# Paged attention behind per-sequence adapters: the order of the work ahead of the first step, and the adapter gathers of the first group, rearranged

## The chip, the cores and the metric

One core of a Trainium2 chip runs the whole kernel. The metric is the device time of one execution in microseconds (us). The kernel before takes 1193.76 us, the median of 3 runs (1192.11 to 1201.34).

## The reference, cut to what matters

There are 8 sequences of 128 tokens with 512 values each, all in float32. First a full 512x512 adapter matrix is picked for each sequence and its product is added; then comes one attention layer with 32 query heads on 8 key heads of 128 values, over 512 cached keys and the 128 new ones.

```python
x = x + einsum('bsi,boi->bso', x, weight[adapter_ids])         # 16 adapters of 512 x 512
q, k, v = x @ Wq.T, x @ Wk.T, x @ Wv.T                         # 32, 8 and 8 heads of 128
q, k = rope(rmsnorm(q, q_norm_w), pos), rope(rmsnorm(k, k_norm_w), pos)   # pos = seqlen + token
kc, vc = k_cache[block_table], v_cache[block_table]            # 16 pages of 32 rows per sequence
scores = q . [kc, k] / sqrt(128), cached keys at or past seqlen masked
x = x + softmax(scores) @ [vc, v] @ Wo.T
```

## The kernel before, in words

**Steps.** The heads are split into G = 4 groups of 2 key heads and 8 query heads. A step is one group of one sequence; 32 steps run in the order group by group, sequence by sequence (`steps`, L248). A step has 8 slots, one for each query head: its score product `sc` (L1040, two matmuls into one of two PSUM buffers), mask and row minimum on DVE (L1050), exponential on ACT (L1066), reciprocal on DVE (L1106), scaling on POOL (L1113), and a 32x32-block transpose on DVE (L886) whose result goes through an exchange of four DMAs on SP's queue (`exchange`, L803) to become `pT`. Between the score products, PE does the pieces of the list `main`: the value product `o` and output product `out` of the step before, and the projections `pj_kv`, `pj_q` of the step after. A planner gives each piece a cost and hands each slot an equal share of what is left (L1093 to L1100).

**Operands.** Every product needs both sides turned. In the first step that is done by PE: four 128x128 transposes into a PSUM buffer (`ps_mm`, four buffers; with `spare` the two score buffers), then a copy out by ACT or DVE (`turn_x` L550, `turn_weights` L492, `turn_lora` L529, `turn_lora_row` L542, `turn_x1` L553, `turn_kc` L756, `turn_k` L768, `turn_q` L787). Later q, k and weights go through DVE transposes and exchanges. `copy_k` (L775) copies the new keys on ACT out of the exchanged `qT` of the step to come; it stands ahead of that slot's exponential in ACT's order.

**Group 0 in particular.** The first eight steps also do the adapters. For step i, sequence i + 2 is turned in slot 0, its adapter in slots 0 to 3 (2 to 5 in step 0), its product `y` comes with `main` (`lora_y`, L587), the addition to the residual follows on DVE (L591), and the sum is turned again by `turn_x1`, registered with `at` for slot 8 of the step, which is slot 0 of the next (slot 9 in step 0). The adapter of sequence b + 3 is gathered by an indirect DMA of 1024 KB that POOL issues (`gather_lora`, L237), in slot 6 (L1128 to L1130) together with the load of x (`load_x`, SP's queue). It lands in a single buffer, the one that `turn_lora` reads. POOL also issues the gathers of cached keys (slots 3 and 5) and values (slots 6 and 7).

**Ahead of step 0** (L932 to L983) the order is written out by hand; each engine takes its own instructions in this order. Two small rows hold sequence lengths and inverse frequencies (the first), and block table, adapter numbers and norm weights (the second). `spread` (L387) brings a row to all partitions by a matmul with ones. `rope_angles` (L394) works the first on DVE; `row_rest` (L423) the second: it casts it, spreads it and makes `bt_f` and `lora_ix` on DVE and `wn` on ACT. From them come the index tables (`row_numbers`, `row_values` on POOL, `row_tables` for groups 1 to 3 on DVE), the sine and cosine (`rope_sin`, `rope_cos` on ACT) and `rope_table` (four DVE operations for keys, five for queries). `pending` is a list of work that follows a product (`rotate`, L644: squares on ACT, then products with the tables on DVE; `norm_scales`, L687: power on POOL, then scaling on ACT); `run(pending)` issues it. A PSUM buffer is read by one engine after the other: in the trace DVE's L664 starts only when ACT's squares of the same product are done.

The order of the hand-written part before, PE's view: the first row, x of sequence 0, value weights (kv 2, 3), key weights (kv 0, 1), the second row, the four adapter blocks, `y`, first query weights (q0 0, 1), q0 2, 3, x1 of sequence 0, second query weights q1 0, 1, `pj_kv`, `pj_q` 0, the cached keys (`turn_kc`), q1 2, 3, `pj_q` 1, x of sequence 1, its adapter, q, k, and then step 0.

Of the kernel before, what the change touches and what calls it, by code (L numbers as in the profile page):

```python
# [19 lines left out]
B = 8  # L20
# [3 lines left out]
D = 128  # L24
# [28 lines left out]
def lora_then_paged_attention(  # L53
# [204 lines left out]
    for i, (g, b) in enumerate(steps):  # L258
        if i == 0:
            at(i, 2, False, lambda: turn_q(0, 1))  # L260
            at(i, 7, False, lambda: turn_q(1, 0))
            for n, h in enumerate((7, 8, 9, 10)):
                at(i, h, False, lambda n=n: turn_weights(("o1", 0, n)))
        if i == last:
            at(i - 1, 6, False, lambda: turn_q(last, 0))
            at(i, 2, True, lambda: turn_q(last, 1))


        for j, n, slot in ((0, i - 1, 6), (1, i, 2)):
            if (i, 0) in by_pe and i:  # L270
                at(n, slot, bool(j), lambda i=i, j=j: turn_k(i, j), 1)
            elif i:
                at(n, slot + 1 - j, True, lambda i=i, j=j: copy_k(i, j), 0)
            elif j:
                at(n, slot, True, lambda: turn_k(0, 1), 1)
        if g == 0 and b + 2 < B:
            at(i, 0, True, lambda b=b: turn_x(b + 2))
            for c in range(KC):
                at(i, c if i else c + 2, False, lambda b=b, c=c: turn_lora(b + 2, c))
            at(i, 8 if i else 9, True, lambda b=b: turn_x1(b + 2))  # L280
    for turns in turns_at.values():
        turns.sort(key=lambda t: not t[0])

# [110 lines left out]
    def rope_angles():  # L394
        nc.vector.tensor_copy(row_f[:, 0:B], row_i[:, 0:B])
        row = spread(0)
        nc.vector.tensor_copy(len_f, row[:, 0:B])
        par_f = rope["par"] = const.tile([P, 1], FP, name="par_f")
        nc.vector.tensor_copy(par_f, par)
        pos = const.tile([P, B], FP, name="pos")  # L400
        nc.vector.tensor_scalar(pos, len_f, par_f, None, ALU.add)
        def temp(tag):
            n = 4 + GK if tag in ("q0", "tq0") else 4
            t = work.tile([P, n, D], FP, tag=tag, name=f"rope_{tag}")
            return t[:, 0:4, :].rearrange("p h (u d) -> p (h u) d", u=2)

        ang, turns, sin, cos = temp("q0"), temp("q1"), temp("tq0"), temp("sw")
        nc.vector.tensor_tensor(
            ang,
            pos.unsqueeze(2).to_broadcast([P, B, H2]),  # L410
            row[:, at_ivf : at_ivf + H2].unsqueeze(1).to_broadcast([P, B, H2]),
            ALU.mult,
        )
        nc.vector.tensor_scalar(turns, ang, 1.0 / (2 * math.pi), ROUND, ALU.mult, ALU.add)
        nc.vector.tensor_scalar(turns, turns, ROUND, None, ALU.subtract)
        for part in (TWO_PI_1, TWO_PI_2, TWO_PI_3):
            nc.vector.scalar_tensor_tensor(
                out=ang, in0=turns, scalar=-part, in1=ang, op0=ALU.mult, op1=ALU.add
            )
        nc.vector.tensor_scalar(ang, ang, PI_BELOW, -PI_BELOW, ALU.min, ALU.max)  # L420
        rope.update(ang=ang, sin=sin, cos=cos)

    def row_rest():  # L423

        nc.vector.tensor_copy(row_f[:, at_bt:at_wn], row_i[:, at_bt:at_wn])
        row = spread(1)
        nc.vector.tensor_copy(rows_of["bt_f"].rearrange("p c q -> p (c q)"), row[:, 0:NB])
        nc.vector.scalar_tensor_tensor(
            out=lora_ix,
            in0=row[:, NB : NB + B],  # L430
            scalar=float(HID // 4),
            in1=rope["par"].to_broadcast([P, B]),
            op0=ALU.mult,
            op1=ALU.add,
        )
        for n in range(2):
            lo = at_wn - at_bt + (1 - n) * D
            nc.scalar.copy(wn[:, n, :], row[:, lo : lo + D])
# [10 lines left out]
        nc.scalar.activation(cos, cos, AF.Sin)  # L449
        table_set(AF.Exp)  # L450

    def rope_table(n):
        sin, cos = rope["sin"], rope["cos"]
        if n == 0:


            nc.vector.tensor_scalar(wn[:, 0, :], wn[:, 0, :], -SCALE, None, ALU.mult)
        w1 = wn[:, n, 0:H2].unsqueeze(1).to_broadcast([P, B, H2])
        w2 = wn[:, n, H2:D].unsqueeze(1).to_broadcast([P, B, H2])
        nc.vector.tensor_tensor(SW[:, n, :, H2:D], sin, w1, ALU.mult)  # L460
        nc.vector.scalar_tensor_tensor(
            out=SW[:, n, :, 0:H2], in0=sin, scalar=-1.0, in1=w2, op0=ALU.mult, op1=ALU.mult
        )
        nc.vector.tensor_tensor(CW[:, n, :, 0:H2], cos, w1, ALU.mult)
        nc.vector.tensor_tensor(CW[:, n, :, H2:D], cos, w2, ALU.mult)

# [462 lines left out]
    on_act, on_vec = nc.scalar.copy, nc.vector.tensor_copy  # L931
    row_parts()  # L932
    table_set(AF.Sin)
    rope_angles()
    turn_x(0, on_act)
    for n in (2, 3, 0, 1):
        turn_weights(("kv", 0, n), on_act)
    rope_sin()
    row_rest()
    for j in range(4):  # L940
        turn_lora_row(0, j, (on_act, on_vec)[j % 2])
    row_numbers()
    for c in range(LC):
        gather_k(0, c)
    row_values()
    rope_cos()
    for _, f in lora_y(0):
        f()
    rope_table(1)
    for n in range(2):  # L950
        turn_weights(("q0", 0, n), on_act)
    flush()
    for n in range(2, 4):
        turn_weights(("q0", 0, n), on_act)
    turn_x1(0, on_vec)
    for n in range(2):
        turn_weights(("q1", 0, n), on_act)
    make_mask(0)
    for _, f in project(0, "kv"):
        f()  # L960
    rope_table(0)
    run(pending)
    for _, f in project(0, "q0"):
        f()
    run(pending)
    for j in range(GK):
        turn_kc(0, j, on_vec)
    for n in range(2, 4):
        turn_weights(("q1", 0, n), on_act)
    run(pending)  # L970
    for c in range(LC):
        gather_k(1, c)
    row_tables(range(1, G))
    for _, f in project(0, "q1"):
        f()
    turn_x(1, on_vec)
    for c in range(KC):
        turn_lora(1, c, on_vec if c % 2 else on_act, True)
    gather_lora(2)
    turn_q(0, 0, on_act)  # L980
    turn_k(0, 0, on_act)
    for _ in range(3):
        load_next()  # L983

# [2 lines left out]
    for i, (g, b) in enumerate(steps):  # L987
        s = st[i]
        main = []
        if i == 0:  # L990
            main += lora_y(1)

            def second(n):
                run(pending)
                if n == 2:
                    turn_x1(1)
                turn_weights(("o0", 0, n))

            main += [(4 * TR * (1 + n // 2), lambda n=n: second(n)) for n in range(3)]
            main += [(4 * TR, lambda: turn_weights(("o0", 0, 3)))]  # L1000
        early = i >= B - 2
        if i and not early:
            main += values(i - 1, 0)
# [25 lines left out]
        for h in range(8):  # L1029
# [86 lines left out]
            if i < last:  # L1116
# [8 lines left out]
                    gather_v(i + 1, c)  # L1125
                if h == 6:
                    pending.append(lambda i=i: make_mask(i + 1))
            if g == 0 and h == 6 and b + 3 < B:  # L1128
                load_x(b + 3)
                gather_lora(b + 3)  # L1130
            if 8 * i + h - 1 in turn_when:
                load_next()

# [57 lines left out]
```

## Time and profile before

| | |
|---|---|
| median of 3 runs | 1193.76 us (1192.11 to 1201.34) |
| the profiled execution | 1193.18 us, of which the span from first to last instruction is 1191.3 us |
| granted TensorE clock over the span | 0.999 |
| busy: PE, DVE, POOL, ACT | 1172.7, 743.9, 674.1, 534.0 us |
| DMA moved | 217.59 MB, mean 183 GB/s |
| first score product of step 0 | at 40.75 us |
| first score products of steps 1 to 6 | at 74.14, 116.13, 160.87, 201.33, 241.80 and 282.26 us |

How to read it: times are us from the first instruction. A busy PE is one that has a matmul in flight, also where the matmul runs at half clock; "A <- B: 2.4, 1, 2.4" in the table of waits is the time that A's engine stood idle until B was done, in total, how often, and the longest. A timeline row is start, duration, engine, line, operation, written tile <- read tiles, and in brackets the idle time before it.

### The profile page before, as it was taken

Reading aid. Unit: us, or ns where it says so; the run is one execution under the profiler, and the core shown is the slowest. Engines: PE = TensorE matmul, PEld = TensorE weight load, DVE = VectorE, ACT = ScalarE, POOL = GpSimd, SP = SyncE. Lnnn points to the kernel's source line nnn. Section 1 sums busy time; section 2 is a strip of 40 time slices with the busy share of each in tenths; the row PEclk is TensorE's granted clock in tenths of the full one; section 3 lists DMA queues with packets and bytes.
Section 4 is the critical chain, followed back from the end, with each engine's and each line's share of the span. In section 5 each row is a group of like instructions: output and inputs, shape, how many; then the busy total and the mean of one; then the engine's idle time right before and its main releaser. Section 6 shows DMA issues by size and latency. Waiting matters only on the chain.

```text
span 1191.3 us, 13375 instructions
## 1 busy us (share of the span) xinstructions
PE 1172.7 (98%) x3354; PEld 572.0 (48%) x3354; DVE 743.9 (62%) x1675; ACT 534.0 (45%) x1648; POOL 674.1 (57%) x780
## 2 busy tenths in 40 slices
PE   7899999999999999999999999999999999999998
PEld 4555454454444444444444444444444444444454
DVE  5566566565667676666666676676666656665651
ACT  4564444444444444444444444444444444444432
POOL 5565346455666565656655556565555656655540
PEclk9999999999999999999999999999999999999999
DMA  8277577766867977786777978766777875665642
GB/s 291 100 180 197 135 220 206 172 180 168 226 173 189 253 192 191 191 215 169 199 187 180 258 198 216 196 175 171 190 203 178 219 180 148 148 153 135 152 111 59
DMA packets 173952, 217.59 MB, mean 183 GB/s; under 512 B 19508, under 2 KB 112436, under 8 KB 172980
## 3 DMA queue, kind: packets, MB, share of 16 engines
q1 hardware_dynamic: 111072, 128.76, 46.8%
q10 hardware_dynamic: 49524, 48.12, 12.7%
q0 software_dynamic: 13280, 39.86, 10.4%
q8 instruction: 28, 0.46, 0.2%
q14 instruction: 48, 0.39, 0.1%
HBM read 80.74 MB, written 17.83 MB: 83 GB/s over the span
## 4 chain that ended last, share of the span: by engine, by line
PE 96%; POOL 1%; DMA 1%; ACT 1%; DVE 1%; issue 1%; DVEq 0%; ACTq 0%; POOLq 0%
PE sc L1040 23%; PE o L566 23%; PE pj_q L566 18%; PE out L566 18%; PE pj_kv L566 9%; PE y L566 2%; PE lw L481 1%; DMA lraw<-in_L_cond_weight_dram,lora_ix 1%; PE x L481 1%; PE wt_q L499 0%; PE wt_kv L499 0%; PE qt L793 0%; PE wt_o L499 0%; POOL kc L617 0%; POOL vc L617 0%
## 5 line engine op out<-in xcount | busy, mean ns | idle before, releaser
L1050 DVE CUSTOM_DVE_ANT_0 p<-sc,mask 128x640 f32<-128x640 f32 x256 | 210.9, 824 | 381.2 <-PE sc L1040 380.9
L1066 ACT ACTIVATE p<-p,mn 128x640 f32<-128x640 f32 x256 | 212.0, 828 | 331.8 <-DVE mn L1050 328.0
L1113 POOL TENSOR_SCALAR p<-p,rc 128x640 f32<-128x640 f32 x252 | 201.5, 800 | 235.3 <-DVE rc L1106 230.9
L1040 PE MATMUL sc<-kT,qT 128*128 128x512 f32 (+1 forms) x1024 | 319.5, 434 | 1.1 <-ACT kT L773 0.8
L1040 PEld LDWEIGHTS sc<-kT,qT 128*128 128x128 f32 x1024 | 192.7, 191 | 232.5 <-issue 225.7
L566 PE MATMUL pj_q<-w_q,x1T 128*128 128x512 f32 x512 | 236.8, 593 | 0.7 <-ACT w_q L500 0.7
L566 PE MATMUL o<-pT,vc 128*128 128x512 f32 x512 | 237.1, 593 | 0.0
L566 PE MATMUL out<-w_o,oT 128*128 128x512 f32 (+1 forms) x528 | 234.9, 580 | 0.9 <-ACT oT L853 0.7
L886 DVE STREAM_TRANSPOSE tp<-p 128x640 f32<-128x640 f32 x252 | 210.8, 837 | 4.0 <-POOL p L1113 3.8
L685 POOL TENSOR_TENSOR q<-q,sw 128x512 f32<-128x512 f32 (+1 forms) x89 | 96.6, 1086 | 98.8 <-DVE sw L668 98.6
L617 POOL DMA_INDIRECT kc<-in_L_cond_k_cache_dram,key_ix x128 | 130.7, 1021 | 32.7 <-issue 32.5
L617 POOL DMA_INDIRECT vc<-in_L_cond_v_cache_dram,val_ix x128 | 127.3, 995 | 31.2 <-issue 29.8
L566 PEld LDWEIGHTS out<-w_o,oT 128*128 128x128 f32 x528 | 95.7, 190 | 93.5 <-issue 85.4
L566 PEld LDWEIGHTS pj_q<-w_q,x1T 128*128 128x128 f32 x512 | 92.4, 190 | 92.7 <-issue 90.6
L698 ACT ACTIVATE q<-q,rs 128x128 f32<-128x128 f32 x256 | 81.8, 390 | 118.1 <-POOL q L685 102.2
L566 PEld LDWEIGHTS o<-pT,vc 128*128 128x128 f32 x512 | 92.2, 191 | 88.5 <-issue 86.4
L566 PE MATMUL pj_kv<-w_kv,x1T 128*128 128x512 f32 x256 | 116.6, 593 | 0.7 <-ACT x1T L483 0.7
L651 ACT ACTIVATE sq<-pj_q 128x128 f32<-128x128 f32 x256 | 70.6, 276 | 57.5 <-PE pj_q L566 41.6
L693 POOL TENSOR_TENSOR rs<-ss,mhalf 128x6 f32<-128x6 f32 x64 | 77.3, 1207 | 5.3
L566 PEld LDWEIGHTS pj_kv<-w_kv,x1T 128*128 128x128 f32 x256 | 46.0, 190 | 45.6 <-issue 44.7
L566 PE MATMUL o<-pT,vn 128*128 128x512 f32 x128 | 65.4, 593 | 0.0
L651 ACT ACTIVATION_READ_ACCUMULATOR sq<-pj_q 128x1 f32 x256 | 49.7, 194 | 0.0
(123 smaller groups left out, 811.5 us busy)
## 6 DMA issues: line engine op xcount, KB each, us to landing
pT<-tp SPq DMA_DIRECT2D x252, 320.0 KB, 6.1
kT<-tk SPq DMA_DIRECT2D x248, 64.0 KB, 2.9
qT<-tq SPq DMA_DIRECT2D x116, 96.0 KB, 2.7
qT<-tq SPq DMA_DIRECT2D x120, 64.0 KB, 4.0
st_q<-in_L_cond_Wq_dram ACTq DMA_DIRECT2D x24, 256.0 KB, 5.5
xw_q<-tw_q ACTq DMA_DIRECT2D x24, 256.0 KB, 5.5
st_o<-in_L_cond_Wo_dram ACTq DMA_DIRECT2D x24, 256.0 KB, 5.7
xw_o<-tw_o ACTq DMA_DIRECT2D x24, 256.0 KB, 6.5
```

Source lines behind the costliest of these rows:

```text
L481: nc.tensor.transpose(t[:, j, :], blk, ident)
L566: nc.tensor.matmul(y[0], lhsT=lhsT, rhs=rhs, start=(k == 0), stop=(k == len(pieces) - 1))
L617: nc.gpsimd.indirect_dma_start(out=dst[:, c, :], out_offset=None, in_=src, in_offset=bass.IndirectOffsetOnAxis(ap=rows[:, g, at : at + 1], ...
L651: nc.scalar.activation(sq, t[:, h, :], AF.Square, scale=float(D) ** -0.5, accum_out=ss[:, h : h + 1])
L685: add.tensor_tensor(dst, cw, sw[:, 0:heads, :], ALU.add)
L693: nc.gpsimd.tensor_tensor(rs[:, 0:width], ss[:, 0:width], mhalf[:, 0:width], ALU.pow)
L698: nc.scalar.activation(q, q, AF.Identity, scale=rs[:, h : h + 1])
L886: nc.vector.transpose(u.tp[:, :, r, :], u.p.pop(r).rearrange("q (a k) -> q a k", a=4))
L1040: nc.tensor.matmul(sc[:, lo:hi], lhsT=s.qT[j][:, r, 0:4, :].rearrange("d h q -> d (h q)"), rhs=s.kT[j].rearrange("d a c i -> d (a c i)")[: ...
L1050: nc.vector.tensor_tensor_reduce(out=p, in0=sc[:, 0:LA], in1=mask.rearrange("p a c i -> p (a c i)"), scale=1.0, scalar=3.0e38, op0=ALU.add ...
L1066: nc.scalar.activation(p, p, AF.Exp, bias=unit.mn[:, one], scale=-1.0, accum_out=unit.sm[:, one])
L1113: nc.gpsimd.tensor_scalar(q, p, unit.rc[:, one], 1.0, ALU.mult, ALU.mult)
```

## The change

Nothing is computed otherwise. The diff reorders:

- Ahead of step 0: x of sequence 0 and the key weights kv 0, 1 are turned before the first row is spread, value weights kv 2, 3 after it. The second row's cast stands amid `rope_angles`, and its spread between the second and the third adapter block; the first two blocks are both copied by ACT. Sine and cosine come after the index tables. `x1` of sequence 0 is turned after q0 0, 1 and not after q0 2, 3. The key table is made in two halves around it. q1 2, 3 stand after `pj_kv`; `pj_q` 1 follows `pj_q` 0 directly, its rotation is issued there and not in step 0; the cached keys' turn comes after that, and the gather of the next cached keys stands ahead of that turn. k is turned ahead of q. The mask comes after `pj_q` 0.
- Step 0: the four output weights o0 are turned before x1 of sequence 1, which stood between the second and the third. `row_tables` moves to slot 6.
- Group 0: in steps 1 to 4, x of sequence b + 3 is loaded in slot 4 and its adapter gathered in slot 5 (both slot 6 before; step 0 keeps slot 6). x1 of the last sequence is turned in slot 7 of step 5, not in slot 0 of step 6.

```diff
+            at(i, 6, False, lambda: row_tables(range(1, G)), 0)
...
-            at(i, 8 if i else 9, True, lambda b=b: turn_x1(b + 2))
+            at(i, (7 if b + 3 == B else 8) if i else 9, True, lambda b=b: turn_x1(b + 2))
...
         nc.vector.tensor_scalar(turns, turns, ROUND, None, ALU.subtract)
+        nc.vector.tensor_copy(row_f[:, at_bt:at_wn], row_i[:, at_bt:at_wn])
         for part in (TWO_PI_1, TWO_PI_2, TWO_PI_3):
...
     def row_rest():
-        nc.vector.tensor_copy(row_f[:, at_bt:at_wn], row_i[:, at_bt:at_wn])
...
-    def rope_table(n):
+    def rope_table(n, parts=("sin", "cos")):
...
     row_parts()
     table_set(AF.Sin)
+    turn_x(0, on_act)
+    for n in range(2):
+        turn_weights(("kv", 0, n), on_act)
     rope_angles()
-    turn_x(0, on_act)
-    for n in (2, 3, 0, 1):
+    for n in range(2, 4):
         turn_weights(("kv", 0, n), on_act)
-    rope_sin()
+    for j in range(2):
+        turn_lora_row(0, j, on_act)
     row_rest()
-    for j in range(4):
+    for j in range(2, 4):
         turn_lora_row(0, j, (on_act, on_vec)[j % 2])
     row_numbers()
     for c in range(LC):
         gather_k(0, c)
     row_values()
+    rope_sin()
     rope_cos()
     for _, f in lora_y(0):
         f()
-    rope_table(1)
+    rope_table(1, ("sin",))
     for n in range(2):
         turn_weights(("q0", 0, n), on_act)
     flush()
+    turn_x1(0, on_vec)
     for n in range(2, 4):
         turn_weights(("q0", 0, n), on_act)
-    turn_x1(0, on_vec)
+    rope_table(1, ("cos",))
     for n in range(2):
         turn_weights(("q1", 0, n), on_act)
-    make_mask(0)
     for _, f in project(0, "kv"):
         f()
+    for n in range(2, 4):
+        turn_weights(("q1", 0, n), on_act)
     rope_table(0)
     run(pending)
     for _, f in project(0, "q0"):
         f()
+    make_mask(0)
     run(pending)
-    for j in range(GK):
-        turn_kc(0, j, on_vec)
-    for n in range(2, 4):
-        turn_weights(("q1", 0, n), on_act)
+    for _, f in project(0, "q1"):
+        f()
     run(pending)
     for c in range(LC):
         gather_k(1, c)
-    row_tables(range(1, G))
-    for _, f in project(0, "q1"):
-        f()
+    for j in range(GK):
+        turn_kc(0, j, on_vec)
     turn_x(1, on_vec)
     for c in range(KC):
         turn_lora(1, c, on_vec if c % 2 else on_act, True)
     gather_lora(2)
+    turn_k(0, 0, on_act)
     turn_q(0, 0, on_act)
-    turn_k(0, 0, on_act)
...
             def second(n):
                 run(pending)
-                if n == 2:
+                if n < 4:
+                    turn_weights(("o0", 0, n))
+                else:
                     turn_x1(1)
-                turn_weights(("o0", 0, n))
...
-            main += [(4 * TR * (1 + n // 2), lambda n=n: second(n)) for n in range(3)]
-            main += [(4 * TR, lambda: turn_weights(("o0", 0, 3)))]
+            main += [(4 * TR, lambda n=n: second(n)) for n in range(5)]
...
-            if g == 0 and h == 6 and b + 3 < B:
-                load_x(b + 3)
-                gather_lora(b + 3)
+            if g == 0 and b + 3 < B:
+                if h == (4 if i else 6):
+                    load_x(b + 3)
+                if h == (5 if i else 6):
+                    gather_lora(b + 3)
```

In the diff, `rope_table` also gets two `if` lines that choose between its two sine operations and its two cosine operations.

## The prediction

> **What bounds the kernel now.** The page first, for who is busy; then the table of PE's waits, for what can be won at all; then busy time by stretches, for the clock behind one of those waits; last the timeline of each wait.
>
> ```profile
> PE 1172.7 (98%) x3354; PEld 572.0 (48%) x3354; DVE 743.9 (62%) x1675; ACT 534.0 (45%) x1648; POOL 674.1 (57%) x780
> ```
>
> PE is the bound: no other engine is near, and the change removes no PE work. The span of 1191.3 us holds 18.6 us of PE idleness, 4.0 of it behind 1160 us, where nothing is changed. So a gain of 1% (11.9 us) is nearly out of reach, and 1% is also about what a measurement of this kernel can tell from no change.
>
> ```profile
> PE spread L391 <- DVE row_f L395: 6.1, 1, 6.1
> PE lw L481 <- DMA lraw<-in_L_cond_weight_dram,lora_ix: 2.4, 1, 2.4
> PE x L481 <- DVE rc L1106: 0.9, 1, 0.9
> PE wt_q L499 <- ACT w_q L500: 0.9, 1, 0.9
> PE y L566 <- DVE wT L483: 0.9, 1, 0.9
> PE sc L1040 <- ACT kT L773: 0.8, 1, 0.8
> PE spread L391 <- ACT w_kv L500: 0.8, 1, 0.8
> ...
> PE pj_kv L566 <- ACT x1T L483: 0.7, 1, 0.7
> PE pj_q L566 <- ACT w_q L500: 0.7, 1, 0.7
> ```
>
> Each is one wait, so each can be put to its place: the start, the row's spreads, `y`, q1's copies and `sc` lie ahead of step 0; `x <- rc` is x1 of sequence 1 in step 0 (DVE's addition of `y` runs 47.74 to 48.80); `lw <- lraw` is the gathered adapter at 120.8 to 123.2, in step 2; `pj_kv <- x1T` is x1 of sequence 7 at the head of step 6.
>
> ```profile
> 119.89:123.30 3.41, 1.01 (x4) 0.21 (x3) 1.32 (x3) 0.74 (x2) 1.76 (x2) 1.00 0.57 179
> 123.30:126.71 3.41, 3.41 (x9) 2.17 (x10) 0.29 (x1) 0.59 (x1) 0.00 (x0) 0.50 0.09 22
> 126.71:130.00 3.29, 3.29 (x10) 1.40 (x9) 1.47 (x4) 0.92 (x2) 0.80 (x1) 1.00 0.36 103
> ```
>
> Columns: stretch, its length, busy time of PE, its weight loads, DVE, ACT, POOL, granted clock, DMA share, GB/s. The wait for the adapter is dearer than its 2.4 us: PE was busy for 1.01 of 3.41 us, and then the clock was 0.50 for 3.41 us, in which PE, fully busy, did half its work. That is 1.7 us more.
>
> **Part by part.** *Adapter gathers one slot sooner.* The one that was late:
>
> ```profile
> 106.23 0.97 POOL L617 DMA_INDIRECT kc<-in_L_cond_k_cache_dram,key_ix  x1 [0.30 <-issue]
> 110.39 0.80 POOL L1113 TENSOR_SCALAR p<-p,rc 128x640 f32<-128x640 f32 x1 [3.19 <-DVE rc L1106]
> ...
> 113.95 0.95 POOL L239 DMA_INDIRECT lraw<-in_L_cond_weight_dram,lora_ix  x1 [0.30 <-issue]
> ```
>
> It lands 9.1 us after its issue. In slot 5 it is issued behind the key gathers, at 107.5, in POOL's idle stretch before 110.39, so no scaling is held up; its buffer was read last at 94.8. Even with 9.1 us it lands at 116.6, four us early. Gone: 2.56 us from the start of the last matmul to the first transpose, less its own time, and 1.67 of clock: -4.2.
>
> The Trainium skill, "TensorE: Matmul & The Clock Gate" (section "Why this matters for your kernels"), puts the drop of the clock at idle gaps over about 3 us. The row above shows it after 2.4 us of idleness, so the measurement decides; by the page this wait would be worth 2.6, not 4.2, and the total 1.6 less.
>
> What the gather collides with is the exchange of the next step's q, which runs in slots 5 to 7 and feeds `copy_k` on ACT ahead of the next step's first score product:
>
> ```profile
> 159.17 0.43 ACT L778 COPY kT<-qT 128x128 f32<-128x128 f32 x1 [3.46 <-DMA qT<-tq]
> 159.49 0.84 ACT L1066 ACTIVATE p<-p,mn 128x640 f32<-128x640 f32 x1
> ```
>
> Step 3's first product starts at 160.87, so this copy has 1.27 us of room; steps 4 and 5 have 1.46 (199.87 to 201.33) and 1.69 (240.11 to 241.80), step 2 has 3.73 (112.40 to 116.13). No row shows gather and exchange side by side in full. Bounds for the delay of the exchange: 0, if they share without loss (no gain, since the exchange had the queues nearly to itself before), and 2.7 us, the whole gather at the 390 GB/s that it gets at 161 to 163 us. By the packet records about 100 of 512 q packets are left when the gather's would begin in step 2, 80 in step 3, 400 in step 4: 6, 5 and all 8 turns on each of 16 DMA engines, with 8 KB packets of a third of a us each. So 2.0, 1.7 and 2.7 late, less the room: 0.7 + 0.2 + 1.0 = +1.9; between 0 and 3.7. Behind the waiting copy stand that slot's exponential and, through its sum, a reciprocal on DVE; PE needs neither within the slot of 4.5 to 5 us.
>
> The Trainium skill, "DMA: Bandwidth & Descriptors" (section "Queues, rings and completion order"), says that each DMA engine goes round between the queues at packet granularity, which speaks against this edit; it is an estimate from the page's 27 GiB/s that eight 8 KB packets hold an engine for 2.3 us, by which these stalls would be 2.7 at most, where the rows above give up to 3.7.
>
> x in slot 4 puts a 256 KB load on SP's queue ahead of the pT exchange. SP waits there for DVE (pT's first DMA is issued at 144.69, the load's slot begins at 140.23), so it costs nothing; without that gap, 0.9 us of issue, inside the room above.
>
> *x1 of sequence 7 in slot 7 of step 5.* Its sum is done at 268.17 and the slot begins at 277.75, so it waits for nothing, and its copy is done long before `pj_kv`. The 0.7 and the 0.2 of refilling go: -0.9. If the copy's cover were gone, the same 0.9 would come back.
>
> *o0 ahead of x1 of sequence 1.* Two turns of 0.43 each move into the wait for the addition (47.74 to 48.80): of 1.09 us lost, -0.8 to -1.0. I take -0.8, since the fourth turn may wait 0.2 for a PSUM buffer. `row_tables` (0.75 of DVE) in slot 6 lies beside a DVE that is idle over 1 us in each slot: 0.
>
> *Ahead of step 0*, chained with the durations of before. x has landed at 3.6 and Wk at 4.5 (packet records), so x and Wk turn from 3.6 to 6.2 at the half clock of the start (0.85 each), 2.4 us sooner; the spread follows at 6.2 (6.06 before), the angles end at 11.9 (11.54). Then the lead is partly lost: the second half of the adapter lands at 11.95, its turns end at 12.9; `lora_ix` is at 12.2 (13.06), `wn` on ACT behind it at 12.7, and the last copies of adapter blocks end at 13.2 (ACT) and 13.8 (DVE). `y` starts at about 13.9, 1.5 sooner than 15.44. It ends 3.6 later, but x1 now has only two weight turns (0.87) ahead of it instead of four, and the addition takes 1.11: 0.5 of waiting. `pj_kv`: about 1.0 sooner (21.3 for 22.29). q1's last two turns (0.87) lie between products now, copied during `pj_q` 0, so the waits of 0.88 and 0.67 go and `pj_q` 1 ends at 32.7 instead of 36.6.
>
> But `sc` needs more than PE:
>
> ```profile
> 31.09 0.69 DVE L664 TENSOR_TENSOR q<-pj_q,CW 128x512 f32<-128x512 f32 x1 [3.20 <-ACT sq L651]
> 31.70 0.74 DVE L668 TENSOR_TENSOR sw<-pj_q,SW 128x256 f32<-128x256 f32 x2
> 32.48 0.69 DVE L685 TENSOR_TENSOR q<-q,sw 128x512 f32<-128x512 f32 x1
> 33.08 1.28 DVE L766 COPY kT<-kct 128x512 f32<-128x512 f32 x2
> ```
>
> `pj_q` 0 ends when it did (29.3), so its squares (1.57 on ACT), these rows (2.08) and its scaling (1.28) end at 34.4 as before. Now a second rotation is issued there: squares to 36.0, DVE rows to 38.1, and only then the keys' copies (to 39.3), x's and the adapter's. On PE the third adapter turn waits for an ACT copy behind the squares (36.6). The fourth waits for a score buffer: ACT's copy of the third (37.8) or DVE's of the second (40.5). The trace gives buffers out as they come free, not in turn: at 31.58 q1's fourth turn started on ACT's copy of the third, while DVE read the product before until 32.44. So 37.8, then k and q, their copies (0.38 and 0.58), and `sc` at 40.0 instead of 40.75: -0.8. Bounds: -1.5, if the lead of `y` is kept to the end, and +1.7, if DVE's copy is waited for (42.4). The rotation of query half 1 is then missing in step 0 on ACT and DVE, where it was beside PE's work: 0. POOL waits with the next keys' gathers until about 37.6 (33.0 before) and gathers adapter 2 at 42.8 instead of 39.6; it lands by 49.1 with the median 6.3, and its first turn is at 53.57, so 4 us of cover remain.
>
> One risk has no price yet: PE is busy for some 0.9 us between 34.8 and 38.2, about as little as in the row at 119.89. A half clock there costs 0 to 1.7; I take 0, since the stretch that is judged must fall almost exactly there, and keep 1.7.
>
> Sum: -4.2 + 1.9 - 0.9 - 0.8 - 0.8 = -4.8. The profiled execution took 1193.18 (span 1191.3 and 1.9 around it), 0.6 below the median of 1193.76; 1193.2 - 4.8 = 1188.4 beside a profile like it, **1189.0** beside the median.
>
> **Rivals.** *The tail ahead of step 0 turns into a DVE wait.* For it: DVE has rotation, keys, x and adapter copies in one line. Against it: the buffer rule at 31.58. `sc` at 42.4 and a half clock: +2.4 + 1.7, so 1193.1. *The gather is harmless and the front's lead is kept:* for it, room of 1.3 to 1.7 at each head; against it, the round of packets. -1.9 - 0.7: 1186.4. *The gather's gain is not there:* the adapter lands late in step 2 wherever it is issued; for it, 9.1 us against a median of 6.3; against it, 13.2 us from 107.5 to 120.7. Without the 4.2: 1193.2. *Slower: the gather starves the exchange of q.* For it: 768-byte packets against 8 KB ones. If the exchange is late by more than room plus 2.4 us, about 4 us, PE idles long enough to lose its clock as well, 2.6 + 1.67 at each of three heads: 12.8 in place of 1.9, so 1199.9. Against it: the gather alone takes 2.7. It decides from 2.2 us of stall a head on, where three eat the 6.7 of all gains.
>
> **How the numbers follow.** Forecast 0.53 (own range 1187 to 1191), DVE tail 0.20, harmless gather 0.14, no gain from the gather 0.04, starved exchange 0.09. From 1185.5 to 1196 leaves the starved case and little else outside. Over 1% faster (below 1181.8) is beyond every case: 0.02. Over 1% slower (above 1205.7) needs the starved case at several times its price: 0.05. Within 1%: 0.93.
>
> **What would show it.** PE's first instruction near 3.7, `y` near 13.9, `pj_q` 1 right behind `pj_q` 0, `sc` near 40.0. No wait for `lraw` and no clock of 0.50 in step 2. Waits of `sc` on `copy_k` of 0.2 to 1.0 at the heads of steps 3 to 5. Wrong if `sc` starts after 41.5, if the clock drops ahead of step 0, or if a head of a step waits over 2 us.

## The result and the profile after

The changed kernel takes 1202.41 us, the median of 20 runs (1197.27 to 1205.95); the kernel before, over 20 runs, 1194.20 (1191.34 to 1201.34). The ratio is 1.0062, 95% interval 1.0047 to 1.0078: slower, by 0.6%, where a gain of 0.4% was forecast, and outside the range of 1185.5 to 1196.0. The profiled execution of the changed kernel took 1202.10 us (span 1200.0), 8.9 more than that of before.

PE is still the bound, and does not do more: its busy time grew by 6.4 us, most of it because a half clock makes the same work longer (three stretches more at half clock, below).

```profile
PE 1179.1 (98%) x3354; PEld 575.0 (48%) x3354; DVE 743.1 (62%) x1674; ACT 534.1 (45%) x1649; POOL 676.9 (56%) x780
```

In the table of PE's waits, the wait for `lraw` and the one of x1 of sequence 7 are gone, as forecast. In their place stand `sc <- kT` of line 781 (`copy_k`, line 778 before) with 7.0 us in three waits, and the adapter's turn (`lw <- wT`) ahead of step 0:

```profile
PE sc L1047 <- ACT kT L781: 7.0, 3, 3.1
...
PE lw L484 <- ACT wT L486: 2.2, 2, 1.5
PE sc L1047 <- DVE wT L486: 0.9, 1, 0.9
```

The three waits are at the heads of steps 2, 3 and 5. Between the starts of two matmuls, less the first one's own time, they cost 1.46 (from 118.45), 2.70 (from 160.49) and 3.30 us (from 245.90). The first score products of steps 1 to 7 start at 76.89, 120.34, 163.61, 205.87, 249.63, 292.32 and 326.72; from there on the two kernels run in step, 8.7 us apart.

Busy time by stretches, of the changed kernel, shows the rest (PE busy, its weight loads, DVE, ACT, POOL, granted clock, DMA share, GB/s):

```profile
11.45:14.86 3.41, 2.54 (x13) 1.45 (x12) 2.00 (x5) 2.53 (x7) 1.46 (x6) 1.00 1.05 401
14.86:18.27 3.41, 3.41 (x5) 1.33 (x4) 1.68 (x3) 2.26 (x4) 2.67 (x7) 0.50 1.07 418
38.75:42.17 3.42, 1.61 (x11) 0.94 (x9) 3.39 (x7) 1.55 (x3) 2.86 (x3) 1.00 0.14 38
42.17:45.58 3.41, 3.17 (x9) 2.17 (x10) 1.35 (x3) 1.28 (x4) 2.57 (x3) 0.50 0.86 288
...
246.97:250.38 3.41, 0.75 (x2) 0.49 (x3) 0.34 (x1) 1.21 (x4) 0.00 (x0) 1.00 0.09 28
250.38:253.79 3.41, 3.41 (x12) 2.47 (x11) 2.48 (x6) 2.39 (x8) 2.61 (x3) 0.50 0.09 31
```

Each pair is a stretch in which PE waits and the stretch behind it, at clock 0.50. There are four such pairs (the fourth is 161.63 to 168.46), where before had one. A full PE at half clock loses 1.7 us in 3.41.

The account, profiled execution against profiled execution: ahead of step 1 +2.75 (first score product +1.66, half clock +1.6, o0 ahead of x1 -0.4); heads of steps 2, 3, 5 +7.46; half clock behind two of them +3.4; the wait for `lraw` and its half clock -4.2; x1 of sequence 7 -0.8. That makes +8.6 of 8.9.

Where the three waits come from is seen at the head of step 5. In the kernel before, `copy_k` waits 3.25 us there for the exchanged q and is done at 240.11, 1.69 us ahead of the product:

```profile
239.68 0.42 ACT L778 COPY kT<-qT 128x128 f32<-128x128 f32 x1 [3.25 <-DMA qT<-tq]
```

In the changed kernel the gather is issued at 238.57, `copy_k` waits 8.20 us and PE stands for 3.14:

```profile
238.57 0.95 POOL L239 DMA_INDIRECT lraw<-in_L_cond_weight_dram,lora_ix  x1 [0.30 <-PE pj_q L569]
...
249.17 0.41 ACT L781 COPY kT<-qT 128x128 f32<-128x128 f32 x1 [8.20 <-DMA qT<-tq]
...
249.63 0.70 PE L1047 MATMUL sc<-kT,qT 128*128 128x512 f32 x1 [3.14 <-ACT kT L781]
```

From the end of the last issue of the exchange to the end of `copy_k` it took 3.7 us there before and 8.6 now; in steps 1 and 2, 3.9 and 5.3 before, 8.8 and 8.6 now; in step 3, 5.4 and 5.5. The packet records say how: in step 1 the gather's 128 packets of 8 KB start from 112.2 to 118.7, 6.5 us and not 2.7, with a mean of 0.41 us each. In the kernel before, the exchange of that step starts up to 155 of its 768-byte packets in half a microsecond; beside the gather it starts mostly 4 to 12, to 6 to 25 of the gather's. They also say why the head of step 4 does not wait: when the gather's first packet starts, 259, 168, 41 and 490 of the exchange's 512 packets are still to come in steps 1 to 4, so the exchange of step 3, which feeds that head, was nearly over.

The tail ahead of step 0 in the timeline of the changed kernel:

```profile
37.39 0.28 ACT L654 ACTIVATE sq<-pj_q 128x128 f32<-128x128 f32 x1
...
37.79 0.69 DVE L667 TENSOR_TENSOR q<-pj_q,CW 128x512 f32<-128x512 f32 x1 [2.46 <-ACT sq L654]
38.29 0.66 PE L484 MATMUL lw<-ident,lraw 128*128 128x128 f32 x4 [1.52 <-ACT wT L486]
...
39.62 0.65 PE L484 MATMUL lw<-ident,lraw 128*128 128x128 f32 x4 [0.68 <-ACT wT L486]
...
41.59 1.28 DVE L486 COPY wT<-lw 128x512 f32<-128x512 f32 x2
42.41 1.19 PE L1047 MATMUL sc<-kT,qT 128*128 128x512 f32 x1 [0.90 <-DVE wT L486]
```

ACT's adapter copy, for which the turn at 38.29 waits, stands behind the last of the squares (37.39); DVE's copies of cached keys, x and adapter stand behind the rotation that begins at 37.79, and the first score product waits for the first of the two adapter copies (done at 42.27). PE waits 1.68 and 0.84 for the last two turns.

### The profile page after: what moved, and what is told of

It is laid out like the page before. It is cut to its first block, busy times and chain, and to the rows that moved or that the text cites. A ratio compares the mean times of both kernels' runs of the same rounds, so it can differ in the third digit from the quotient of the medians.

```text
span 1200.0 us, 13377 instructions
## 1 busy us (share of the span) xinstructions
PE 1179.1 (98%) x3354; PEld 575.0 (48%) x3354; DVE 743.1 (62%) x1674; ACT 534.1 (45%) x1649; POOL 676.9 (56%) x780
## 4 chain that ended last, share of the span: by engine, by line
PE 93%; SPq 2%; DMA 2%; DVE 1%; issue 1%; ACT 1%; POOL 0%; ACTq 0%; DVEq 0%; POOLq 0%
PE o L569 23%; PE sc L1047 22%; PE pj_q L569 17%; PE out L569 17%; PE pj_kv L569 9%; SPq L809 2%; PE y L569 2%; DMA qT<-tq 1%; PE lw L484 1%; PE x L484 1%; ACT sq L654 0%; PE wt_q L502 0%; DMA kT<-tk 0%; PE wt_kv L502 0%; DVE tp L889 0%
## 5 line engine op out<-in xcount | busy, mean ns | idle before, releaser
L1113 DVE RECIPROCAL rc<-sm 128x1 f32<-128x1 f32 x256 | 33.4, 131 | 28.3 <-ACT p L1073 25.2
```

The source lines that it names most:

```text
L1113: nc.vector.reciprocal(unit.rc[:, one], unit.sm[:, one])
```

## The experiments

Two questions: which part costs the time, and by what mechanism. The theory after the result was that the gather's packets hold up the exchange of q, and that the second rotation ahead of step 0 holds up the copies behind it, both with the clock on top. The rivals: that the earlier load of x on SP's queue delays the exchange; that all comes from the part ahead of step 0; that the start varies by itself. Each kernel was run 6 to 12 times, and its ratio is taken against 20 to 35 runs of the kernel before that were made beside it (medians 1192.80 to 1194.27), so the ratios can be compared and the medians of different rows less so.

| kernel | median us | against before, with 95% interval |
|---|---|---|
| gathers and loads sooner, nothing else | 1199.48 | 1.0048 (1.0029 to 1.0066) |
| loads of x in slot 4 alone | 1191.04 | 0.9998 (0.9980 to 1.0015) |
| gather in slot 5 in step 1 alone | 1191.70 | 0.9999 (0.9984 to 1.0013) |
| gather of step 1 first in slot 6 | 1190.82 | 0.9981 (0.9967 to 0.9996) |
| changed kernel, gathers back in slot 6 | 1194.56 | 1.0016 (0.9999 to 1.0033) |
| new order ahead of step 0 alone | 1195.90 | 1.0013 (0.9997 to 1.0028) |
| first half of that order alone | 1194.46 | 1.0003 (0.9986 to 1.0019) |
| second half of it alone | 1197.11 | 1.0025 (1.0007 to 1.0044) |
| second half, rotation left to step 0 | 1191.14 | 0.9983 (0.9966 to 1.0000) |
| gather in slot 5, 64 partitions | 1196.12 | 1.0011 (0.9994 to 1.0027) |
| gather in slot 5, four of 2 KB rows | 1193.47 | 1.0002 (0.9986 to 1.0018) |
| gather in slot 5, four of 32 partitions | 1200.17 | 1.0061 (1.0040 to 1.0082) |
| first half, eight transposes added | 1194.54 | 1.0014 (0.9999 to 1.0029) |
| what helped, put together | 1186.87 | 0.9942 (0.9923 to 0.9962) |
| the same with the filled first half | 1186.38 | 0.9951 (0.9931 to 0.9971) |

### The gather or the load

On the kernel before:

```diff
-            if g == 0 and h == 6 and b + 3 < B:
-                load_x(b + 3)
-                gather_lora(b + 3)
+            if g == 0 and b + 3 < B:
+                if h == (4 if i else 6):
+                    load_x(b + 3)
+                if h == (5 if i else 6):
+                    gather_lora(b + 3)
```

> The kernel before with only the loads of x in slot 4 and the adapter gathers in slot 5 of steps 1 to 4; nothing ahead of step 0 is touched. Theory A (the gather's packets hold up the exchange of q, which copy_k and the next step's first score product wait for): the wait for lraw and the half clock behind it go (-4.2), and the heads of steps 2, 3 and 5 wait 1 to 4 us each, as in the changed kernel (1.5 + 2.7 + 3.3 there), with two stretches of clock 0.50 (+3.4): +6 to +7 us in all. Theory B (the earlier load of x on SP's queue is what makes the exchange late): the same time here, so this run does not tell A from B; the next one does. Theory C (gather and load are harmless, and all of the loss comes from the part ahead of step 0): -4.2 us and no head waits over 0.5.

Measured: +0.48%, +5.7 us. Heads of steps 2, 3 and 5 wait 1.72, 1.41 and 3.30, and two stretches of 0.50 lie behind the last. In the table of waits:

```profile
PE sc L1040 <- ACT kT L778: 5.9, 3, 3.1
```

This alone is most of the loss of the changed kernel; theory C falls.

The same with `h == 6` for the gather:

> The kernel before with only the loads of x moved to slot 4; the gathers stay in slot 6. Theory A (gather): within 1 us of before, the wait for lraw in step 2 stays at 2 to 2.6 us, no head of steps 2 to 5 waits over 0.5 for copy_k. Theory B (load): the heads wait as in the changed kernel, 7 us and up to 3.4 of clock, so +7 to +11 us.

Measured: no difference, no head waits. Theory B falls: the load is harmless. The wait for `lraw` in step 2 is 0.9 in this execution and not the 2 to 2.6 that were expected.

In step 1 alone (`h == (5 if i == 1 else 6)` for the gather, load in slot 6):

> The kernel before with the gather in slot 5 in step 1 alone, the only one that landed late; the loads of x and the other gathers stay in slot 6. Theory A: the wait for lraw and its half clock go (-4.2), the head of step 2 waits 1.0 to 2.5 for copy_k because that one exchange is held up, the heads of steps 3 to 5 do not wait: -1.5 to -3 us. Theory B: -4.2 us, with no wait at any head.

Measured: 0.9999, less than expected. The head of step 2 waits 1.21 and the adapter's wait in step 2 is gone (one of 0.7 stands in step 4, whose gather was not moved); what the one gives the other takes. As theory A has it in kind; the -4.2 proved too large (below).

The gather of step 1 only one place sooner, ahead of the value gathers of slot 6:

```diff
+                if i == 1 and h == 6:
+                    gather_lora(b + 3)
                 for c in {6: (0, 1), 7: (2, 3)}.get(h, ()) if i else (range(LC) if h == 7 else ()):
                     gather_v(i + 1, c)
...
-                gather_lora(b + 3)
+                if i != 1:
+                    gather_lora(b + 3)
```

> The kernel before with the gather of step 1 issued in slot 6 as before, but ahead of that slot's two gathers of values and not behind them: about 2.6 us sooner (near 111.3), when the packets of the exchange of q have just ended (111.3 in the trace of before). Theory A: it lands by about 120.5, the wait for lraw shrinks from 2.4 to under 0.5 and its half clock goes, no head waits: -3.5 to -4.2 us. Rival: the gather takes its time from what else is moved then (values, keys' exchange), lands no sooner, and the wait stays: within 1 us of before.

Measured: -0.19%, -2.2 us; neither PE's wait for `lraw` nor a wait for `copy_k` is in the table any more. The mechanism holds, the size is half.

### Why the gather holds the exchange up

Half the partitions:

```diff
+        half = P if b < 4 else P // 2
         nc.gpsimd.indirect_dma_start(
-            out=lraw[b],
+            out=lraw[b][0:half, :],
```

> As the run with the gathers in slot 5 (1.7, 1.4 and 3.3 us of wait at the heads of steps 2, 3 and 5), but the adapters of sequences 4 to 7 are gathered for 64 of 128 partitions only: half the bytes and packets, same issue, same place; the other half of these adapters keeps what the buffer held, so part of the computation is left out. Theory A (the gather's packets hold the exchange off for as long as they run): the waits at the heads fall to under half, 0 to 1.5 us each, no clock of 0.50 there, the time is -3 to 0 us against before. Rival (it is the order of issue on POOL or SP's queue, not the bytes): the waits stay at 1.4 to 3.3 us, +4 us or more.

Measured: +0.11% against +0.48% for the whole gather, so half a gather costs less. But in the profiled execution, the longest of its 12 (1203.9), the heads of steps 2, 3 and 5 wait 0.30, 2.92 and 4.06. There the 64 packets took 0.53 to 0.68 us each, where the 128 of the whole gather took 0.34 to 0.42 in the run before. Neither theory as written: fewer packets, but longer ones.

Four gathers of a quarter of each row:

```diff
+        for j in range(4):
+            nc.gpsimd.indirect_dma_start(
+                out=lraw[b][:, HID * j : HID * j + HID],
+                in_=lora_w.rearrange("m r i -> (m r) i"),
+                in_offset=bass.IndirectOffsetOnAxis(ap=lora_4[:, j, b : b + 1], axis=0),
```

> As the run with the gathers in slot 5, but each gather from step 1 on is four gathers of 2 KB rows (512 packets of 2 KB for 128 of 8 KB); POOL issues four DMAs of about 1 us each. Theory A with turns per packet (between two packets of the exchange stands one or two of the gather, whatever their size): packets of a quarter of the size let the exchange go about four times as fast, the head waits fall to under 1 us: -3 to +1 us, where POOL's 4 us of issue may delay its scaling. Rival (bytes: the gather takes its share of the bandwidth, whatever the packets): the waits stay at 1.5 to 3 us per head, +4 us or more.

Measured: 1.0002, no wait at any head. The records show packets of 4 KB (256 for a gather, not the 512 of 2 KB that were expected), 0.19 to 0.21 us each. In the timeline of this run the last of the four gathers of step 4 is issued at 237.06, and the copy is done half a microsecond ahead of the product, which waits for nothing:

```profile
237.06 0.95 POOL L248 DMA_INDIRECT lraw<-in_L_cond_weight_dram,lora  x1 [0.31 <-issue]
...
240.08 0.43 ACT L794 COPY kT<-qT 128x128 f32<-128x128 f32 x1 [4.36 <-DMA qT<-tq]
...
241.08 1.13 PE L1056 MATMUL sc<-kT,qT 128*128 128x512 f32 x3
```

The exchange is free, but the four gathers are not. They keep POOL for 4.7 us in step 3 (150.39 to 155.08), where one issue took 0.9, and ACT's scaling of q, which waits for POOL, and its copy of x behind it come late; in steps 3 and 4 PE waits for that copy, 1.2 us each time. The waits of PE, and ACT in step 3:

```profile
PE lw L497 <- ACT x1T L499: 2.3, 2, 1.2
```

```profile
161.25 1.28 ACT L714 ACTIVATE q<-q,rs 128x128 f32<-128x128 f32 x4 [5.37 <-POOL q L701]
162.44 1.04 ACT L499 COPY x1T<-x 128x512 f32<-128x512 f32 x2
```

That takes back what the earlier gather gives, which fits 1.0002.

These gathers differ in two ways, size of packets and pace. So the pace alone, with rows of 8 KB (`out=lraw[b][32 * j : 32 * j + 32, :]`, four times):

> As the run with the gathers in slot 5, but from step 1 on each gather is four gathers of 32 partitions with rows of 8 KB, issued as fast as the four gathers of 2 KB rows were. All four take the first 32 indices, so the adapters of sequences 4 to 7 are not the right rows; bytes and place are the same. Theory S (size of the packets: an engine that has an 8 KB packet of the gather in hand keeps the exchange's 768-byte ones waiting, about one for one): the waits at the heads come back, 1 to 3.5 us at two or three of the heads of steps 2 to 5, +3 us or more against before. Theory T (pace: a gather that comes in four parts leaves gaps for the exchange): no head waits over 0.5 us, within 1.5 us of before, as with the four gathers of 2 KB rows (0.0%).

Measured: +0.61%. The waits come together at one head, that of step 5 (timeline; the four gathers are issued from 231.37 to 235.74):

```profile
245.73 0.41 ACT L788 COPY kT<-qT 128x128 f32<-128x128 f32 x1 [11.95 <-DMA qT<-tq]
...
246.18 1.22 PE L1050 MATMUL sc<-kT,qT 128*128 128x512 f32 x1 [6.88 <-ACT kT L788]
```

Pace does not help; theory T falls. One head and not two or three waits, so theory S has the sum and not the pattern. It is not a clean pair either: rows on 32 partitions make packets of 0.58 to 0.61 us. So what stands is: with packets of 0.2 us no head waits, with 0.34 to 0.42 three heads wait up to 3.3, and the two runs with packets of 0.6 us have the longest single waits, 4.1 and 7.0. At which head they fall is not settled. The Trainium skill, "DMA: Bandwidth & Descriptors" (section "Queues, rings and completion order"), has each DMA engine go round between queues one packet at a time, where a packet may hold several descriptors. The half-microsecond counts do not settle the turns: about two packets of the gather to one of the exchange in step 1, and about one to one in steps 2 and 4. Which engine held which packet the records do not say.

### Ahead of step 0

The changed kernel with `load_x` and `gather_lora` back in slot 6:

> The changed kernel with loads of x and adapter gathers back in slot 6; the part ahead of step 0, o0 ahead of x1 of sequence 1 and x1 of sequence 7 in slot 7 stay. Theory A (the gathers in slot 5 cost the time): the waits at the heads of steps 2, 3 and 5 go, 5 to 6 us less than the changed kernel, so about +1 to +2.5 us against before, all of it from the part ahead of step 0. Rival (the part ahead of step 0 costs as much as the gathers): still +4 us or more.

Measured: +0.16%: theory A. Its trace has `sc` at 42.46 and clock 0.50 from 42.15, as the changed kernel has.

The kernel before with the hand-written part of the changed one:

> The kernel before with the changed kernel's order ahead of step 0 and row_tables in slot 6 of step 0; steps and gathers as before. Theory P (the order itself costs time): first score product near 42.4 where before has 40.75, a stretch of clock 0.50 ahead of or behind it, +2 to +3.4 us. Rival V (the start varies from run to run by itself: with the order of before it is at 40.75, 40.76, 43.63 and 45.56 in four profiled executions, by when the clock comes up): within 1 us of before over many runs.

Measured: +0.13%, or 1.5 us, between the two, with an interval that just takes in zero; both first score product (44.54) and clock (0.50 from 44.17) are as theory P has them, but this execution came up late (clock 1.00 only from 20.27), which is rival V's point. So it was split at `pj_kv`.

> The kernel before with only the first half of the new order (up to the turn of q1 0 and 1); from pj_kv on it is as before. Forecast's chain: y 1.5 sooner, pj_kv 1.0 sooner, first score product near 39.8: -1 us. Theory P, as the changed kernel's trace has it: y starts near 14.4 but runs at half clock, pj_kv no sooner than 22.3, first score product 41 to 42: 0 to +1.5 us.

Measured: 1.0003. Theory P: `y` starts at 13.75 and takes 5.4 us in place of 3.7, and the lead is gone.

> The kernel before with only the second half of the new order (from pj_kv on, row_tables in slot 6 of step 0). Forecast's chain: about 0 (the waits on q1's copies go, the wait behind the second rotation takes their place). Theory P: pj_q 1 ends 1.5 to 2 sooner, but the tail from there to the first score product takes 7 to 8 us instead of 4.3, because the copies of cached keys and adapter stand behind the rotation of pj_q 1 on ACT and DVE; first score product 1.5 to 2 later, and 1.6 more where the clock drops: +1.5 to +3.5 us.

Measured: +0.25%. The waits of 1.68 and 0.84 at the adapter's turns are there, and 6.8 us of clock 0.50 from 40.09. Then the same with the second `run(pending)`, and the gathers of the next cached keys behind it, ahead of `pj_q` 1:

```diff
     for _, f in project(0, "q0"):
         f()
     make_mask(0)
     run(pending)
+    run(pending)
+    for c in range(LC):
+        gather_k(1, c)
     for _, f in project(0, "q1"):
         f()
-    run(pending)
-    for c in range(LC):
-        gather_k(1, c)
     for j in range(GK):
         turn_kc(0, j, on_vec)
```

> The kernel before with the second half of the new order, but the rotation of pj_q 1 left to step 0, as before: it is issued behind the copies of cached keys and adapter and not ahead of them. Theory R (the loss of the second half is those copies standing behind the rotation on ACT and DVE, and the clock that PE loses while it waits for them): the waits on the third and fourth adapter turn (1.68 and 0.84 in the run with the second half alone) and the clock of 0.50 behind them go, while the two waits on q1's copies (1.05 and 0.84 in before) stay away; first score product about 1 us sooner than before for the same start of y: -0.5 to -1.5 us. Rival (the loss is in the cached keys' turn behind pj_q 1, wherever the rotation is): still +1.5 us or more.

Measured: -0.17%, first score product at 38.77 where before has 40.75 in an execution with `y` at the same place; the two waits are 0.40 and 0.27, and no clock of 0.50. The wait on ACT's adapter copies in the two tables, with the rotation there and without it:

```profile
PE lw L482 <- ACT wT L484: 2.2, 2, 1.5
```

```profile
PE lw L482 <- ACT wT L484: 0.2, 1, 0.2
```

Theory R: the second rotation is the loss, and a loss of 3.0 us turns into a gain of 2.0 without it (the interval of the gain just reaches zero; against the loss it is clear). The key gathers moved with the call, but the waits that went are on ACT's copies and not on these gathers.

### The clock in the first half

> The kernel before with the first half of the new order, as in the earlier run of it, and eight transposes more on PE (0.87 us of work that nobody reads) in the wait of 1.04 us ahead of y. Theory G (the clock is set by PE's work in the 3.41 us stretch before: 1.30 to 1.36 us there in the new order, just under a bound near 1.4): with 0.87 more in it no clock of 0.50 follows the stretch ahead of y, y takes about 3.7 us and not 5.4, the first score product comes near 39.5, where it was 40.95 with the half clock: -1 to -2 us in the median against the run without the added transposes, -0.5 to -1.5 against before. Rival (the half clock there has another cause, or the lead is lost behind y in any case): the same time as without them, within 0.5 us of before.

In the profiled execution it does what theory G says. Of the first half alone, and then with the added transposes, the stretch ahead of `y` and that of `y`:

```profile
10.78:14.19 3.41, 2.45 (x12) 1.45 (x12) 2.50 (x6) 2.21 (x7) 1.16 (x5) 1.00 1.01 377
14.19:17.61 3.42, 3.42 (x5) 1.35 (x4) 1.68 (x3) 2.64 (x5) 2.81 (x7) 0.50 1.09 417
```

```profile
10.89:14.31 3.42, 3.42 (x21) 2.41 (x21) 2.21 (x6) 2.49 (x7) 1.38 (x6) 1.00 1.01 384
14.31:17.72 3.41, 3.41 (x13) 1.69 (x12) 1.97 (x4) 2.34 (x4) 2.67 (x7) 1.00 1.07 411
```

First score product 39.23 for 40.95. But the median is 1194.54 for 1194.46: no gain over the runs. And 8 of 12 runs of the first half alone have a mean clock of 1.000, where one stretch of half clock shows as 0.998 or 0.999, and yet take 1190.6 to 1197.5. (The mean leaves out the time before the clock first rises: the run with the gather of step 1 first in slot 6 has 1.000, though its clock first rose at 22.61.) So the profiled half clock is not what keeps the first half from paying in the median, or not alone; by its own measure theory G fails there, and why the first half gains nothing stays open.

### Together

What helped, on the kernel before: gather of step 1 first in slot 6, loads of x in slot 4, x1 of sequence 7 in slot 7, o0 ahead of x1, the second half of the order with the rotation left to step 0.

> The kernel before with what the runs leave standing: the gather of step 1 first in slot 6 (-2.2 measured), loads of x in slot 4 (within 0.2% of before, lower median), x1 of sequence 7 in slot 7 of step 5 (its wait of 0.84 goes), o0 ahead of x1 of sequence 1 (-0.4), and the second half of the new order with the rotation of pj_q 1 left to step 0 (-1 by theory R). Theory: -4 to -5 us, ratio about 0.996. Rival (the parts gave what they gave by the start's spread alone): within 1 us of before.

Measured: 0.9942, or 6.9 us (the interval is 4.5 to 9.2): the rival falls, and the gain is if anything larger than the theory's 4 to 5. In steps 0 to 6 no wait for `copy_k`, `lraw` or x1 is left. The changed kernel with the gathers mended, the rotation left to step 0 and the added transposes:

> The changed kernel with three edits: the adapter gathers back in slot 6 (the one of step 1 first in the slot), the rotation of pj_q 1 left to step 0, and eight added transposes ahead of y. Theory G: 1 to 2 us under the same kernel with the first half of before, which measured 0.9942 of before: 0.993. Rival (the first half gives nothing even at full clock): 0.994 again.

Measured: 0.9951, the same within the intervals (rival). Its table of waits has no `sc <- kT`, and its longest entry behind the first loads is 0.9 in two waits:

```profile
PE sc L1050 <- ACT qT L797: 0.9, 2, 0.7
```

## Why the prediction was wrong, point by point

| step | forecast us | in the changed kernel's trace |
|---|---|---|
| wait for `lraw` and its clock | -4.2 | -4.2 |
| exchange held up by the gather | +1.9 (0 to 3.7) | +7.5 of waits, +3.4 of clock |
| x1 of sequence 7 | -0.9 | -0.8 |
| o0 ahead of x1 of sequence 1 | -0.8 | -0.4 |
| ahead of step 0 | -0.8 (-1.5 to +1.7) | +1.7, and +1.6 of clock |

**The step that failed is the exchange.** The mechanism was named, the place too; the size was wrong by a factor of nearly six (10.9 us with the clock, for 1.9), and the upper bound with it. It rested on "2.7 us, the whole gather at the 390 GB/s", with "8 KB packets of a third of a us each", from a stretch in which the gather had the engines nearly to itself. Beside the exchange and the value gathers it took 6.5 us. The trace of before had a warning: its gather of step 1 took 6.0 us too (packets from 116.57 to 122.59). Delays of 4.9, 3.2, 0.1 and 5.0 us in steps 1 to 4 stand against 0 to 2.7 forecast. The counts of packets left were off as well: 168, 41 and 490 in steps 2 to 4, where 100, 80 and 400 were taken. The 3.73 us of room at step 2, put down as enough, were not. The rival of the starved exchange (1199.9, a chance of 0.09) is what happened in kind, at the heads of steps 2, 3 and 5 and not 3, 4 and 5, with the clock at two of them; the 1202.41 measured lies above even that, because the part ahead of step 0 lost as well; the rival was set aside by "the gather alone takes 2.7", the same figure. The estimate of stalls of 2.7 at most from the page's rate is off too: 2.3 us of delay less the three rooms makes 2.5.

**Ahead of step 0 the chain failed at its head and at the clock.** `y` started at 14.45 (forecast 13.9), but at half clock, and so `pj_kv` came at 23.25 and not 21.3, later than before (22.29). What followed was as forecast, only 1.8 us later: squares to 37.8 (forecast 36.0), DVE's rows to 39.9 (38.1), third adapter turn 38.3 (36.6), fourth 39.6 on ACT's copy (37.8). `sc` came 2.8 behind that turn, not 2.2, since it waited for DVE's first adapter copy: at 42.41, with a half clock behind it, which is the rival of the DVE tail (42.4 and 1.7) in place and price. "I take 0" for the clock was the mistake: all four profiled executions with the second rotation there have the half clock in the tail.

**The -4.2 was one execution's.** In the changed kernel's trace it is gained in full. But in seven other profiled executions with this gather in its old place the wait is 0.9 to 2.0 us and none loses its clock there. Issuing the gather first in its slot, which removes that wait and collides with nothing, measured -2.2. A term read from one trace was twice its mean.

**What held:** the wait on x1 of sequence 7; no wait where the moved loads of x were thought free; PSUM buffers given out as they come free; o0's gain in kind, halved because its fourth turn waits 0.66, until DVE's addition is done, and not 0.2. Over the runs the two large parts add up: +0.48% for the gathers and +0.13% for the order ahead of step 0 make the +0.62% measured, well within their intervals.

## What to carry to other kernels

Before a large transfer is moved beside a small one that the bound engine waits for, price it by how long its packets take in a crowded stretch, not by its bytes at the best rate seen: here 8 KB packets beside 768-byte ones made an exchange 3 to 5 us late in three steps of four, and rows of a quarter of the size left it alone, but took four issues of POOL for one and cost 2.3 us elsewhere. Work that is pulled ahead, like the second rotation here, stands in the queues of engines whose next instructions the bound engine may need first; list those before moving it. A stall's price includes the clock: count PE's work in the 3.41 us around it, and look at more than one execution before a single wait is booked as a gain.

## What the runs showed of the hardware

**The clock has a bound on work, and stretches of fixed length.** In all 17 profiled executions the clock changes on a grid of 3.413 us whose place differs from execution to execution. I summed PE's matmul time at full clock in each stretch (0.43 us for 512 columns, 0.11 for 128, the one-row spreads left out). Of the stretches at full clock, all 15 with under 1.30 us of work were followed by clock 0.50, none of over 5700 with more than 1.45, and four of the six between. Of those at half clock, all 38 under 1.30 stayed there, and all 36 above returned to 1.00. So it is not the length of a gap that decides: work under some 40% of a stretch does. Two waits for an adapter of the same length show it: one of 2.03 us cost the clock, as it lay within one stretch (248.92 to 250.94, second half of the order alone), and one of 2.02 us did not, as the edge of a stretch, at 124.07, divided it (123.66 to 125.68, changed kernel with the gathers back in slot 6). The Trainium skill, "TensorE: Matmul & The Clock Gate" (section "Part 1: The HAM clock gate (the "warmup" mystery)"), has the window of 3413 ns that runs free, and the trace agrees; its condition for the drop, a whole idle window, asks for more idleness than these records did.

**Much of the spread from run to run lies in the start.** In eight profiled executions with the hand-written order of before, the first score product came five times at 40.75 or 40.76, and at 43.61, 43.63 and 45.56: in these three the clock fell back once behind its first rise, or first rose at 22.61 and not near 11. That 4.8 us is over half of the 8 us or so over which runs of one kernel spread, and as much as the edits compared here. What the start did in the runs that were not profiled is not on record.
